# Products of Q's and K's projections accumulated in one PSUM bank, with ScalarE reading the bank between them

## The chip, the cores and the metric

The kernel runs on one core of one Trainium2 chip, all in float32. The metric is the device time of one execution in microseconds. The time before is a median of three runs: 1310.24 us, with 1309.48 and 1314.11 us as the lowest and the highest.

An engine's instructions run in the order of its queue. TensorE (PE in the profile) multiplies into PSUM, which has 8 banks here, each holding one 128x512 float32 tile. VectorE (DVE) and ScalarE (ACT) read PSUM; GpSimd (POOL) works on tiles in SBUF only. The loads and stores that matter here are issued by SyncE (SP).

## The reference, cut to what matters

The reference is a transformer block on two sequences of 512 tokens with 512 features: attention with 32 heads of 128, then a small mixture of experts. What the change touches are the first two of the three projections:

```python
xn = _layernorm(x)                    # (2, 512, 512)
q = rms_norm(xn @ Wq + bq, gq)        # (2, 512, 4096)
k = rms_norm(xn @ Wk + bk, gk)        # (2, 512, 4096)
v = xn @ Wv + bv
```

So for each of Q and K a 512 x 4096 weight meets 1024 tokens, a bias is added for each output column, and the squares of every token's 4096 outputs are summed for the norm.

## The kernel before

**The seven products.** `project` (lines 196 to 305) makes Q, and is called again for K. It works in eight chunks `g` of `GH` = 4 heads (512 output columns). In a chunk the product is a 2 x 2 block product: the weight is cut into `a11`, `a12`, `a21`, `a22` (halves of the input features by halves of the columns), and the tokens of the two sequences (`xTs[0]`, `xTs[1]`) are the other 2 x 2 blocks. Seven block products take the place of eight (Strassen's scheme, in Winograd's form). `weight_sums` (line 185) makes the four sums `s1` to `s4` of weight blocks on POOL, one chunk ahead of use; `token_sums` makes `t1` to `t4` once.

**What a product is.** `product(g, i, a, x, j, tag)` (line 214) takes a PSUM tile from `pt` and issues two matmuls into it (`c` = 0, 1), the first with `start`, for head `j` of the two in a column half. Each float32 matmul is two matmul instructions in the profile, so a chunk is 7 products x 2 heads x 2 x 2 = 56 instructions. `pt` (line 75) takes tiles in turn from two rings, "ps" and "aux", of four banks each.

**How the products become four heads for two sequences.** With the products in the order 1, 2, 6, 7, 4, 5, 3, everything twice, for j = 0 and 1:

- ScalarE copies product 1 with the bias to SBUF: `u1` (line 249, Identity).
- VectorE: product 2 + `u1` is head j of sequence 0 (line 252).
- VectorE: `u2` = product 6 + `u1` (line 280), `u3` = product 7 + `step` + `u2` (line 285; `step` is the difference of the biases of heads j+2 and j).
- VectorE: product 4 + `u3` is head j+2 of sequence 0 (line 290); product 5 + `u3` is head j+2 of sequence 1 (line 296); product 5 + `u2` (line 297); product 3 + that is head j of sequence 1 (line 303).

That is 14 additions on VectorE and 2 copies on ScalarE per chunk, and 14 PSUM tiles, each released when its last reader is done.

**What every finished head causes.** `keep_it` (line 230) squares it on ScalarE (line 237) into a tile of the pool `tmp`, which has four buffers, and POOL adds the square to `accq` or `acck` (line 238). SP stores the head to HBM (line 239; `keptq`, `keptk`). Q's heads lie in a pool of five buffers; K's in two pools of five and seven.

**What else runs in this stretch.** During Q, POOL makes sums of V's weights (`value_sums`, lines 331 to 334), and VectorE makes sums of the output weights (`output_sums`, lines 354 to 357). During K, `between()` runs five times per chunk and makes up to two steps of `scale_some` each time: VectorE scales a stored head of Q (line 382), SP stores it again (`keptqs`, line 383), and after every fourth SP loads four more heads (`four_of`, line 377, 1 MB), which needs the four stores from that buffer to have landed. There are 64 such steps. At the start of chunk `g`, `load_next(g + 1)` loads the next weights (line 91, 1 MB, a pool of two buffers) and POOL makes their sums.

**What sets the order.** PE, VectorE, ScalarE and POOL run in the order of the program text (`IN_ORDER`, line 27). SP isn't in that list: the order of its loads and stores is the framework's planner's, by its own estimates of when each is ready.

**The first two chunks of Q** are opened early by `open_chunk(g, "ps")`, while the second sequence is still being normalized; all others by `open_chunk(g)`, where the tag is `None`.

Of the kernel before, what the change touches and what calls it, by code (L numbers as in the profile page):

```python
# [10 lines left out]
AF = mybir.ActivationFunctionType  # L11
ALU = mybir.AluOpType
AX = mybir.AxisListType

P = 128
# [17 lines left out]
def kernel(ctx: ExitStack, tc: tile.TileContext, x, wq, wk, wv, wo, vecs, rows, wbase, gates, bexp, out):  # L33
# [11 lines left out]
    nc = tc.nc  # L45
# [21 lines left out]
    def tt(name):  # L67
        return tmp.tile([P, 512], F32, tag="tmp", name=name)
# [6 lines left out]
    def pt(name, tag=None):  # L75
        if tag is None:
            tag = ("ps", "aux")[turn_of[0] % 2]
            turn_of[0] += 1
        return psum.tile([P, 512], F32, tag=tag, name=name)
# [8 lines left out]
    def load_w(src, name):  # L88

        w = wpool.tile([P, 4, 512], F32, tag="w", name=name)  # L90
        nc.sync.dma_start(out=w, in_=src.rearrange("(c p) f -> p c f", p=P))
        return w
# [92 lines left out]
    def weight_sums(w, name):  # L185

        a11, a12, a21, a22 = w[:, 0:2, 0:256], w[:, 2:4, 0:256], w[:, 0:2, 256:512], w[:, 2:4, 256:512]
        pairs = [vpool.tile([P, 4, 256], F32, tag="v", name=f"s{i}_{name}") for i in range(2)]
        s1, s2, s3, s4 = out = [t[:, i : i + 2] for t in pairs for i in (0, 2)]
        nc.gpsimd.tensor_tensor(s1, a21, a22, ALU.add)  # L190
        nc.gpsimd.tensor_tensor(s2, s1, a11, ALU.subtract)
        nc.gpsimd.tensor_tensor(s3, a11, a21, ALU.subtract)
        nc.gpsimd.tensor_tensor(s4, a12, s2, ALU.subtract)
        return [a11, a12, a22] + out

    def project(xTs, sums, w_src, bias, step, name, pools, keep, accs, parts, between=lambda: None):

        G = H // GH
        begun = set()
        parts = {0: parts}
        opened = {}
        two = range(2)

        def load_next(g):  # L210
            if g < G:
                parts[g] = weight_sums(load_w(w_src[:, ts(g, GH * P)], f"w_{name}{g}"), f"{name}{g}")

        def product(g, i, a, x, j, tag=None):
            ps = pt(f"p{i}_{name}{g}_{j}", tag)
            for c in range(2):
                nc.tensor.matmul(ps, a[:, c, ts(j, P)], x[c], start=(c == 0), stop=(c == 1))  # L217
            return ps

        def column(v, g, j):  # L220
            return v[:, g * GH + j : g * GH + j + 1]

        def tile_of(what, g, j):
            return opool.tile([P, 512], F32, tag="o", name=f"{what}_{name}{g}_{j}")

        def head(g, b, j):
            pool, tag = pools[j // 2 if len(pools) > 1 else 0]
            return pool.tile([P, 512], F32, tag=tag, name=f"{name}{b}_{g * GH + j}")

        def keep_it(o, g, b, j):  # L230
            h = g * GH + j
            if b not in begun:
                begun.add(b)
                nc.scalar.activation(accs[b], o, AF.Square)
            else:
                sq = tt(f"sq_{name}{b}_{h}")
                nc.scalar.activation(sq, o, AF.Square)  # L237
                nc.gpsimd.tensor_tensor(accs[b], accs[b], sq, ALU.add)  # L238
            nc.sync.dma_start(out=keep[b, h], in_=o)

        def open_chunk(g, tag=None):
            a11, a12 = parts[g][0:2]
            ps1 = [product(g, 1, a11, xTs[0][0:2], j, tag) for j in two]
            ps2 = [product(g, 2, a12, xTs[0][2:4], j, tag) for j in two]
            u1 = opened[g] = [tile_of("u1", g, j) for j in two]

            def leave():
                for j in two:
                    nc.scalar.activation(u1[j], ps1[j], AF.Identity, bias=column(bias, g, j), scale=1.0)
                for j in two:  # L250
                    o = head(g, 0, j)
                    nc.vector.tensor_tensor(o, ps2[j], u1[j], ALU.add)
                    keep_it(o, g, 0, j)

            return leave

        if len(xTs) < B:
            load_next(1)
            leave = open_chunk(0, "ps")
            second = norm_transposed(xs[1], "a1", "aux")  # L260
            leave()
            xTs.append(second())
            leave = open_chunk(1, "ps")
            sums.extend(token_sums(xTs))
            leave()
        t1, t2, t3, t4 = sums
        for g in range(G):
            if g + 1 not in parts:
                load_next(g + 1)
            a11, a12, a22, s1, s2, s3, s4 = parts.pop(g)  # L270
            if g not in opened:
                parts[g] = (a11, a12)
                open_chunk(g)()
                del parts[g]
            u1 = opened.pop(g)
            between()
            u2 = [tile_of("u2", g, j) for j in two]
            for j in two:
                ps = product(g, 6, s2, t2, j)
                nc.vector.tensor_tensor(u2[j], ps, u1[j], ALU.add)  # L280
            between()
            u3 = [tile_of("u3", g, j) for j in two]
            for j in two:
                ps = product(g, 7, s3, t3, j)
                nc.vector.scalar_tensor_tensor(u3[j], ps, column(step, g, j), u2[j], ALU.add, ALU.add)
            between()
            for j in two:
                ps = product(g, 4, a22, t4, j)
                o = head(g, 0, j + 2)
                nc.vector.tensor_tensor(o, ps, u3[j], ALU.add)  # L290
                keep_it(o, g, 0, j + 2)
            between()
            for j in two:
                ps = product(g, 5, s1, t1, j)
                o = head(g, 1, j + 2)
                nc.vector.tensor_tensor(o, ps, u3[j], ALU.add)
                nc.vector.tensor_tensor(u2[j], ps, u2[j], ALU.add)
                keep_it(o, g, 1, j + 2)
            between()
            for j in two:  # L300
                ps = product(g, 3, s4, xTs[1][2:4], j)
                o = head(g, 1, j)
                nc.vector.tensor_tensor(o, ps, u2[j], ALU.add)
                keep_it(o, g, 1, j)
            yield g

# [678 lines left out]
```

## Time and profile before

| What | Value | Where |
|---|---|---|
| Median of the three runs | 1310.24 us (1309.48, 1310.24, 1314.11) | the times |
| Span of the profiled execution | 1306.8 us, mean granted clock 0.996 | the page, first and last instruction; the page gives no other time for this execution |
| PE busy over the span | 1281.5 us (98%) | the page, part 1 |
| DVE, ACT, POOL busy | 982.1, 541.4, 496.8 us (75%, 41%, 38%) | the page, part 1 |
| Q's projection from its third chunk on | 62.2 to 206.6 us | the timeline of PE |
| K's projection | 206.6 to 400.5 us | the timeline of PE |

The span counts from the first to the last instruction of the profiled execution; the median of the runs lies 3.4 us above it. In the timeline a line has the start, the duration, the engine, the line of the kernel, the operation, the output and input tiles and a count; in brackets stands the idle time ahead of it and what ended that. In the table of stretches there are, for each stretch, its length, then the busy time of PE, PEld (weight loads), DVE, ACT and POOL with instruction counts, then the granted clock of PE, the busy share of the DMA engines and their GB/s. In the groups a line has the total busy time, the mean duration of one, and the idle time ahead with what ended it.

A PE that is shown busy is not always a PE at its pace: matmuls overlap, and their durations (592 ns) are longer than their distance (3.43 us for eight, 0.429 us each).

### The profile page before, as it was taken

How to read it: one execution, taken by the hardware profiler on the slowest of the kernel's cores; microseconds unless marked ns; L12 is line 12 of the kernel's file. 1: busy time of each engine (PE TensorE's matmuls, PEld its weight loads, DVE VectorE, ACT ScalarE, POOL GpSimd, SP SyncE). 2: the span in 40 equal slices, each digit the busy share in tenths (PEclk: the TensorE clock that was granted, in tenths of full speed). 3: DMA queues.
4: the chain of work that ended last, by engine and by line, in shares of the span. 5: the costliest groups of instructions: out<-in, count | busy, mean ns of one | idle time of the engine just before them, and what ended most of it. 6: DMA issues, size and time to landing. Idle time of an engine off the chain costs nothing.

```text
span 1306.8 us, 11743 instructions
## 1 busy us (share of the span) xinstructions
PE 1281.5 (98%) x3518; PEld 654.9 (50%) x3518; DVE 982.1 (75%) x1208; ACT 541.4 (41%) x746; POOL 496.8 (38%) x382
## 2 busy tenths in 40 slices
PE   7999999999999999999999999999999999999987
PEld 4444444444444444455555555555555555555453
DVE  7565665888765477888787787878778888888865
ACT  5222222322221144344545445454544556555343
POOL 4789897556763011111122222323223233332102
PEclk9999999999999999999999999999999999999999
DMA  7799979699997765534465566576566565643301
GB/s 291 250 321 311 337 278 312 221 335 330 313 341 266 255 189 183 175 129 129 129 173 174 140 191 165 135 196 170 153 162 184 129 169 129 170 97 81 89 1 64
DMA packets 150335, 257.01 MB, mean 197 GB/s; under 512 B 12160, under 2 KB 41728, under 8 KB 150272
## 3 DMA queue, kind: packets, MB, share of 16 engines
q1 hardware_dynamic: 137312, 232.67, 53.2%
q0 software_dynamic: 12096, 22.03, 10.2%
q10 hardware_dynamic: 864, 1.57, 0.3%
q8 instruction: 28, 0.46, 0.1%
q14 instruction: 35, 0.29, 0.1%
HBM read 149.26 MB, written 84.93 MB: 179 GB/s over the span
## 4 chain that ended last, share of the span: by engine, by line
PE 95%; DVE 2%; DMA 1%; ACT 1%; issue 0%; SPq 0%; ACTq 0%
PE ps L531 17%; PE o L589 17%; PE aux L460 15%; PE p_k L217 15%; PE p_q L217 14%; PE aux L646 12%; PE psy L692 2%; PE f L864 1%; DMA w_q<-in_wq 1%; DMA wo<-in_wo 1%; ACT s L580 1%; PE f L920 1%; PE hg L857 0%; PE aux L563 0%; ACT n_f L157 0%
## 5 line engine op out<-in xcount | busy, mean ns | idle before, releaser
L544 POOL PARTITION_ALL_REDUCE top<-m x64 | 122.2, 1910 | 606.6 <-DVE m L542 606.6
L532 ACT ACTIVATE s<-ps,rk 128x512 f32<-128x512 f32 x256 | 175.8, 687 | 308.5 <-PE ps L531 287.3
L589 PE MATMUL o<-s,v 128*128 128x512 f32 x512 | 230.6, 593 | 3.4 <-ACT s L580 3.4
L531 PE MATMUL ps<-qh,kh 128*128 128x512 f32 x512 | 230.2, 592 | 0.0
L531 PEld LDWEIGHTS ps<-qh,kh 128*128 128x128 f32 x512 | 97.3, 190 | 122.5 <-issue 120.8
L589 PEld LDWEIGHTS o<-s,v 128*128 128x128 f32 x512 | 97.0, 190 | 103.8 <-issue 95.7
L550 DVE TRANSPOSE_TENSOR_REDUCE quarters<-s 128x64 f32<-128x2048 f32 x64 | 147.2, 2300 | 0.0
L577 DVE TENSOR_TENSOR s<-s,top 128x2048 f32<-128x2048 f32 x64 | 146.0, 2282 | 0.0
L541 DVE TENSOR_TENSOR m<-s 128x1024 f32<-128x1024 f32 x64 | 78.0, 1219 | 62.0 <-ACT s L532 62.0
L580 ACT ACTIVATE s<-s 128x2048 f32<-128x2048 f32 x64 | 121.7, 1902 | 5.0 <-DVE s L577 5.0
L460 PE MATMUL aux<-w_v,t 128*128 128x512 f32 x256 | 115.8, 596 | 0.0
L646 PE MATMUL aux<-wr,oh 128*128 128x256 f32 x448 | 103.0, 380 | 0.0
L646 PEld LDWEIGHTS aux<-wr,oh 128*128 128x128 f32 x448 | 84.6, 190 | 23.2 <-issue 12.9
L237 ACT ACTIVATE sq_q<-q 128x512 f32<-128x512 f32 x62 | 38.9, 631 | 135.1 <-DVE q L290 68.1
L238 POOL TENSOR_TENSOR accq<-accq,sq_q 128x512 f32<-128x512 f32 x62 | 81.0, 1308 | 36.1 <-ACT sq_q L237 34.1
L238 POOL TENSOR_TENSOR acck<-acck,sq_k 128x512 f32<-128x512 f32 x62 | 86.2, 1394 | 20.6 <-ACT sq_k L237 17.4
L237 ACT ACTIVATE sq_k<-k 128x512 f32<-128x512 f32 x62 | 38.7, 630 | 132.3 <-DVE k L290 65.4
L460 PE MATMUL aux<-w_v,nT_a 128*128 128x512 f32 x192 | 87.5, 596 | 0.0
L217 PE MATMUL p_k<-t,s_k 128*128 128x512 f32 x192 | 85.0, 592 | 0.0
L217 PE MATMUL p_q<-t,s_q 128*128 128x512 f32 x192 | 85.0, 592 | 0.0
L646 PE MATMUL aux<-wr,s_o 128*128 128x256 f32 x336 | 77.4, 380 | 0.0
L460 PEld LDWEIGHTS aux<-w_v,t 128*128 128x128 f32 x256 | 47.6, 190 | 55.0 <-issue 54.3
(185 smaller groups left out, 1713.0 us busy)
## 6 DMA issues: line engine op xcount, KB each, us to landing
keptq<-q SPq DMA_DIRECT2D x64, 256.0 KB, 6.9
q<-keptq SPq DMA_DIRECT2D x16, 1024.0 KB, 6.4
keptk<-k SPq DMA_DIRECT2D x64, 256.0 KB, 6.5
w_v<-keptw SPq DMA_DIRECT2D x32, 512.0 KB, 3.9
keptqs<-q SPq DMA_DIRECT2D x64, 256.0 KB, 6.6
qh<-keptqs SPq DMA_DIRECT2D x64, 256.0 KB, 3.0
kh<-keptk SPq DMA_DIRECT2D x64, 256.0 KB, 2.7
keptv<-o_v SPq DMA_DIRECT2D x64, 256.0 KB, 3.1
```

The costliest lines, as they stand in the source:

```text
L217: nc.tensor.matmul(ps, a[:, c, ts(j, P)], x[c], start=(c == 0), stop=(c == 1))
L238: nc.gpsimd.tensor_tensor(accs[b], accs[b], sq, ALU.add)
L460: nc.tensor.matmul(ps, x[c][:, ts(t, P)], w[:, c, :], start=(c == 0), stop=(c == 1))
L531: nc.tensor.matmul(ps, kk[i][:, ts(k, P)], qs[i], start=True, stop=True)
L532: nc.scalar.activation(s[:, k, :], ps, AF.Copy, scale=rks[b][:, k : k + 1])
L541: nc.vector.tensor_tensor(m, s[:, 0:2, :], s[:, 2:4, :], ALU.max)
L544: nc.gpsimd.partition_all_reduce(ms[i], m[:, 0, :], P, ReduceOp.max)
L550: nc.vector.tensor_reduce(quarters.rearrange("p k j -> p (k j)"), ss[i].rearrange("p k (j r) -> p (k j) r", r=32), AX.X, ALU.add, apply_tr ...
L577: nc.vector.tensor_tensor(s, s, top.unsqueeze(1).to_broadcast([P, NT, 512]), ALU.subtract)
L580: nc.scalar.activation(ss[i], ss[i], AF.Exp)
L589: nc.tensor.matmul(po, vs[b, c][:, k, ts(j, P)], ss[i][:, k, :], start=(k == 0), stop=(k == NT - 1))
L646: nc.tensor.matmul(ps[:, t, :], a, right_of[i, g][:, j, :], start=(j == 0), stop=(j == 1))
```

## The change

`product` may be given a tile to accumulate onto (`onto`): then its first matmul carries no `start`. In the chunks that are opened without a tag, products 1, 6, 7 and 4 accumulate in the bank of product 1, and ScalarE reads the bank after each of them with the right bias: `u1`, `u2`, `u3` and head j+2 of sequence 0. Product 3 accumulates onto product 5's bank. VectorE keeps three additions per head pair: product 2 + `u1`, product 5 + `u3`, and (5 + 3) + `u2`. The order of the products becomes 1, 2, 6, 5, 7, 4, 3. A chunk takes 6 PSUM tiles, 6 additions on VectorE and 8 copies on ScalarE; squares, stores and matmuls are as many as before. In the first two chunks of Q, `chain` is `None`: there products 6, 7 and 4 share a bank, and VectorE reads it.

```diff
-        def product(g, i, a, x, j, tag=None):
-            ps = pt(f"p{i}_{name}{g}_{j}", tag)
+        def product(g, i, a, x, j, tag=None, onto=None):
+            ps = pt(f"p{i}_{name}{g}_{j}", tag) if onto is None else onto
             for c in range(2):
-                nc.tensor.matmul(ps, a[:, c, ts(j, P)], x[c], start=(c == 0), stop=(c == 1))
+                first = c == 0 and onto is None
+                nc.tensor.matmul(ps, a[:, c, ts(j, P)], x[c], start=first, stop=(c == 1), skip_group_check=True)
             return ps
...
-            u1 = opened[g] = [tile_of("u1", g, j) for j in two]
+            u1 = [tile_of("u1", g, j) for j in two]
+            opened[g] = u1, ps1 if tag is None else None
...
-            u1 = opened.pop(g)
+            u1, chain = opened.pop(g)
+
+            def copied(what, ps, j, shift):
+                u = tile_of(what, g, j)
+                if chain is not None:
+                    nc.scalar.activation(u, ps, AF.Identity, bias=column(bias, g, j + shift), scale=1.0)
+                elif shift:
+                    nc.vector.scalar_tensor_tensor(u, ps, column(step, g, j), u1[j], ALU.add, ALU.add)
+                else:
+                    nc.vector.tensor_tensor(u, ps, u1[j], ALU.add)
+                return u
+
             between()
-            u2 = [tile_of("u2", g, j) for j in two]
+            sum6 = [product(g, 6, s2, t2, j, onto=chain and chain[j]) for j in two]
+            u2 = [copied("u2", sum6[j], j, 0) for j in two]
+            between()
+            ps5 = [product(g, 5, s1, t1, j) for j in two]
+            between()
+            sum7 = [product(g, 7, s3, t3, j, onto=sum6[j]) for j in two]
+            u3 = [copied("u3", sum7[j], j, 2) for j in two]
             for j in two:
-                ps = product(g, 6, s2, t2, j)
-                nc.vector.tensor_tensor(u2[j], ps, u1[j], ALU.add)
-            between()
-            u3 = [tile_of("u3", g, j) for j in two]
-            for j in two:
-                ps = product(g, 7, s3, t3, j)
-                nc.vector.scalar_tensor_tensor(u3[j], ps, column(step, g, j), u2[j], ALU.add, ALU.add)
+                o = head(g, 1, j + 2)
+                nc.vector.tensor_tensor(o, ps5[j], u3[j], ALU.add)
+                keep_it(o, g, 1, j + 2)
             between()
             for j in two:
-                ps = product(g, 4, a22, t4, j)
+                product(g, 4, a22, t4, j, onto=sum7[j])
                 o = head(g, 0, j + 2)
-                nc.vector.tensor_tensor(o, ps, u3[j], ALU.add)
+                if chain is not None:
+                    nc.scalar.activation(o, sum7[j], AF.Identity, bias=column(bias, g, j + 2), scale=1.0)
+                else:
+                    nc.vector.scalar_tensor_tensor(o, sum7[j], column(step, g, j), u1[j], ALU.add, ALU.add)
                 keep_it(o, g, 0, j + 2)
             between()
             for j in two:
-                ps = product(g, 5, s1, t1, j)
-                o = head(g, 1, j + 2)
-                nc.vector.tensor_tensor(o, ps, u3[j], ALU.add)
-                nc.vector.tensor_tensor(u2[j], ps, u2[j], ALU.add)
-                keep_it(o, g, 1, j + 2)
-            between()
-            for j in two:
-                ps = product(g, 3, s4, xTs[1][2:4], j)
+                product(g, 3, s4, xTs[1][2:4], j, onto=ps5[j])
                 o = head(g, 1, j)
-                nc.vector.tensor_tensor(o, ps, u2[j], ALU.add)
+                nc.vector.tensor_tensor(o, ps5[j], u2[j], ALU.add)
                 keep_it(o, g, 1, j)
```

## The prediction, made before the changed kernel was run

> **What bounds the kernel now.** I read first the chain of waits from the start to the end of K's projection (start, duration, engine, tile, line, count), since it shows whether the stretch that is changed waits for anything.
>
> ```profile
> 20.98 185.58 PE p_q L217 x432
> 206.56 24.03 PE p_k L217 x56
> 230.59 1.72 PE ssq L412 x4
> 232.31 168.23 PE p_k L217 x392
> 400.54 5.15 PE aux L460 x12
> ```
>
> From 20.98 to 400.54 us the chain is PE alone. 56 instructions take 24.03 us, 0.429 each, and 392 take 168.23, again 0.429: every chunk runs at one pace, K's as Q's, though VectorE's load differs. The table of stretches says the same:
>
> ```profile
> 170.00:180.00 10.00, 10.00 (x25) 4.48 (x24) 4.98 (x8) 1.92 (x4) 9.74 (x8) 1.00 0.97 280
> 270.00:280.00 10.00, 10.00 (x25) 4.48 (x24) 9.88 (x10) 1.86 (x3) 9.31 (x7) 1.00 1.01 326
> ```
>
> PE is busy throughout; VectorE is half idle in Q and full in K (9.88 of 10 us), and PE doesn't mind. The DMA engines are full too (0.97 and 1.01). So VectorE's 75% of the span is not the limit here, and taking work from it can't shorten a chunk. The question is only whether the change makes PE wait.
>
> **What is removed and added.** The groups of Q's stretch have the prices (total, then mean ns):
>
> ```profile
> L280 DVE TENSOR_TENSOR u_q<-p_q,u_q 128x512 f32<-128x512 f32 x12 | 8.3, 690 | 9.5 <-PE p_q L217 9.5
> L285 DVE SCALAR_TENSOR_TENSOR u_q<-p_q,steps,u_q 128x512 f32<-128x512 f32 x12 | 9.0, 751 | 12.0 <-PE p_q L217 12.0
> L249 ACT ACTIVATE u_q<-p_q,vec 128x512 f32<-128x512 f32 x12 | 8.0, 680 | 3.1 <-PE p_q L217 3.1
> ```
>
> In 14 of 16 chunks VectorE loses 8 additions (lines 280, 285, 290, 297: 2 x (0.69 + 0.75 + 0.69 + 0.68) = 5.6 us per chunk, 79 us in all) and ScalarE gains 6 copies (6 x 0.68 = 4.1 us, 57 us). ScalarE then has 8 x 0.68 + 8 squares x 0.63 = 10.5 us of a chunk's 24.03: room enough. In Q's first two chunks VectorE goes from 14 to 12 additions. Matmuls are as many. Direct gain on the path: 0. The chain excludes more: nothing but PE is on it.
>
> **The new waits on PE.** Products 6, 7 and 4 now wait until ScalarE has read the bank, 3 until VectorE has. Behind such a wait stands all of PE's queue. A product pair takes 8 instructions, 3.43 us, so by the time from a chunk's start (0): 1 from 0, 2 from 3.43, 6 from 6.87, 5 from 10.30, 7 from 13.73, 4 from 17.17, 3 from 20.60. The handoffs come from the timeline:
>
> ```profile
> 19.45 0.81 ACT L157 ACTIVATE n_a<-x,shift_a,rs_a 128x512 f32<-128x512 f32 x1 [0.42 <-DMA wo<-in_wo]
> 20.32 0.42 PEld L159 LDWEIGHTS nt_a<-ident,n_a 128*128 128x128 f32 x4 [0.31 <-ACT n_a L157]
> 113.90 0.69 ACT L249 ACTIVATE u_q<-p_q,vec 128x512 f32<-128x512 f32 x1 [0.37 <-PE p_q L217]
> ```
>
> ScalarE to PE: 20.26 to 20.32, 0.06 us. PE to ScalarE: product 1 of the chunk that starts at 110.27 ends at 113.70, the copy starts at 113.90, 0.20 us. The tightest round trip is 7, `u3`, 4: 7 for the first head ends at 15.45, `u3` runs from 15.65 to 16.34, PE may go at 16.40 and wants to at 17.17, or at 16.74 if its weight load (0.43 us ahead in the timeline) has to wait as well. Spare: 0.3 to 0.8 us, so 0; if the trip were 0.5 us longer than these rows, up to 0.2 us per chunk, 3 us in 14 chunks. `u2` has 2.6 us to spare, product 3 more than 3 us. Banks: 6 tiles per chunk in rings of 8, each ring coming round after a chunk and a third; 0. The first two chunks, with VectorE in the loop: `u2` is done near 32.2 us and 7 starts at 34.73; 0.
>
> A rule against this change is in the Trainium skill, ScalarE: Activation LUTs, "Rules for kernel authors": additions belong on VectorE, which is up to about 3x faster in bf16. The rows here are float32 and say 0.68 us against 0.69. An estimate by the rule's factor, 3 x 0.69 = 2.07 us for `u3`, would overrun the spare time by about 1 us per chunk, 14 us in all; by the rows it is 0.
>
> **Where ScalarE is late.** ScalarE is in order, so `u1` stands behind the squares of the chunk before. A square needs a buffer of `tmp` (four), which POOL frees; POOL, in order too, stands before `weight_sums`, which wait for 1 MB of weights. In K's last chunks this already happens:
>
> ```profile
> 365.50 0.67 SPq L91 DMA_DIRECT2D w_k<-in_wk  x1
> ...
> 375.72 1.76 POOL L190 TENSOR_TENSOR s_k<-w_k 128x512 f32<-128x512 f32 x1 [11.38 <-DMA w_k<-in_wk]
> ...
> 381.23 14.22 POOL L238 TENSOR_TENSOR acck<-acck,sq_k 128x512 f32<-128x512 f32 x10
> ...
> 382.52 0.63 ACT L237 ACTIVATE sq_k<-k 128x512 f32<-128x512 f32 x1 [11.42 <-POOL acck L238]
> ```
>
> POOL waits 11.38 us for the weights, ScalarE 11.42 us for POOL. `u1` of the last chunk (line 249) follows at 387.09, 10.6 us after the chunk's start (376.50). Before, only VectorE waited for it; now product 6, due at 383.37, does. The four squares left over need four additions of POOL: 381.23 + 4 x 1.42 + 0.1 + 0.63 = 387.6, `u1` until 388.3, so product 6 would start 5.0 us late. The same sum for the two chunks before: sums done at 328.97 and 352.22, product 6 possible 7.2 us later, at 336.2 and 359.4; due at 335.3 and 359.3: 0.9 and 0.1 us. These don't add up: time that PE lost earlier comes off what it loses later. So 5.0 us with all other times unchanged.
>
> Two things take from it. VectorE no longer blocks POOL so much (POOL's addition is 1.27 us where it is alone, 1.42 here: 4 x 0.15, and some 0.5 over the four sums, 1 us together). And the traffic of K, which fills the DMA engines from about 255 us, can begin earlier: VectorE's first scalings no longer stand among additions (0 to 3 us). One thing adds: SP's order is the planner's, and product 4, which frees the weights' buffer, is now sixth and not fifth (3.43 us later). If the planner puts the load one pair of stores later, past a load that waits for landings (3.5 to 4.5 us in SP's timeline), the sums come 2 to 6 us later. Bounds: 5.0 - 4 = 1, or 0 if a wait further up is lifted, to 5.0 + 6 = 11. I take 3, nearer to the unchanged row less its reliefs.
>
> At the joint of Q and K, VectorE's first head of K waits until 217.43 for POOL's sums of V's weights. Its squares on ScalarE (to 219.4) now stand ahead of `u2`, done at 220.1, and 7 is due at 220.3. Q's last store chain may be 0.9 us later, as head j+2 of sequence 1 is now third in its five buffers: 0 to 0.9 us, and it comes off the 3 later.
>
> **Sum.** 1306.8 (span) + 0 (additions) + 0 (round trips) + 3 (K's `u1`) = about 1310 us of span; the runs' median lies 3.4 above the span, so 1313 us. What is behind K, the values and attention, isn't changed.
>
> **Rivals.**
> (a) *K paced by SP and DMA: slower.* The weight loads of K's chunks 3 to 7 start at 261.83, 287.96, 314.12, 339.07 and 365.50: one per 25.9 us, against 24.03 of PE. Now PE hangs on that pace through `u1`. Place: product 6 in the last three chunks; price: the full bound of 11 us, 1321; it decides once the last sums are done later than about 383 us. For: DMA shares near 1. Against: the reliefs, and that the lag is bounded by what K's stores and loads need anyway.
> (b) *The round trips are longer than the rows: slower.* One overrun per chunk, 14 times; 0.5 us of it makes 7 us, 1317. Against: 0.3 to 0.8 us spare.
> (c) *Nothing waits: unchanged, 1310.* For: squares wait less as POOL speeds up.
> (d) *The relief of VectorE shortens K: faster.* At most what PE idles before 400 us after its start, which the chain has as 0, so only a shift of loads elsewhere could give it; 1303 would take 7 us from the start or the tail, which don't change.
>
> The Trainium skill, TensorE: Matmul & The Clock Gate, "A second HAM failure mode: psum-queue depth-cycling", says that short PE idles between groups that cycle through banks can throttle the clock again. The granted clock here is 1.00 in every stretch before 1256 us, so no run here shows it; an estimate by that page, with each throttled stretch half its time lost, would put several us on top of (a) or (b).
>
> **How the numbers follow.** A measurement of this kernel tells about 0.5% (6.5 us) from no change. Unchanged within that, 0.61: my forecast (0.41, 0.5 to 6.5 us lost) with (c) (0.20). Slower, 0.34: (a) 0.23, (b) 0.11. Faster (d), 0.05. The time is the forecast's, 1313. The range takes the lower end from (c), less 2 us of the runs' own scatter, 1308, and the upper from (a), 1321.
>
> **What would show it.** After: additions on VectorE 6 per chunk, VectorE's busy time down by about 80 us, ScalarE's up by 57. The chain through Q still PE alone, 24.03 us per chunk (the round trips). In K a PE or weight load waiting for ScalarE at line 249 or the read of `u1`, in the last two or three chunks, behind POOL and `w_k`; K's end at 401 to 407 us and the rest of the span shifted by as much. Wrong would be: gaps ahead of product 4 in each chunk (b); K's end past 408 (a); a K that ends before 400 (d).

## The result, and the profile after

| | before | after |
|---|---|---|
| Median of the runs | 1309.86 us (1307.83 to 1314.11, 4 runs) | 1320.87 us (1318.36 to 1323.11, 4 runs) |
| Span of the profiled execution | 1306.8 us | 1321.3 us |
| K's projection ends | 400.5 us | 415.8 us |

The ratio is 1.0075, with a 95% interval from 1.0052 to 1.0097: the change costs 0.5 to 1%, some 11 us. The profiled execution of after took 1323.11 us, the longest of the four, and its span grew by 14.5 us; the medians differ by 11.0. So the sums below, which are made against the profiled execution, explain 3.5 us more than the medians show. The kernel before scatters as well: beside the experiments it ran 23 or 24 times each, with medians from 1310.92 to 1312.58 us, and against these the changed kernel loses 8 to 10 us.

The first part of the changed kernel's page (busy time, share of the span, instructions):

```profile
PE 1286.6 (97%) x3518; PEld 655.5 (50%) x3518; DVE 905.1 (69%) x1092; ACT 593.3 (45%) x830; POOL 493.0 (37%) x382
```

VectorE lost 77 us of work (from 982.1) and ScalarE gained 52 (from 541.4), as the change says. The time went the other way. The chain of waits of the changed kernel, in K's second half (start, duration, what, line, count), cut to its main pieces, where the kernel before had one piece of PE alone from 232.31 to 400.54:

```profile
321.40 9.34 DMA w_k<-in_wk
330.88 1.28 POOL s_k L190
...
342.47 10.53 PE p_k L218 x20
354.57 8.37 DMA keptqs<-q
...
375.58 9.44 DMA w_k<-in_wk
...
394.07 1.27 POOL acck L239
396.72 19.10 PE p_k L218 x40
415.82 5.15 PE aux L471 x12
```

Read its second part downwards: a store lands (354.57), SP gets on and loads weights, POOL makes their sums and adds squares, and only then PE goes on. Twice PE hangs on the end of that chain, at 342.47 and at 396.72. The timeline of PE in the changed kernel (start, duration, engine, line, operation, tiles, count, idle time ahead) has these two and a third:

```profile
216.19 12.23 PE L218 MATMUL p_k<-t,s_k 128*128 128x512 f32 x24 [2.21 <-ACT u_k L251]
243.71 10.46 PE L218 MATMUL p_k<-t,s_k 128*128 128x512 f32 x24
342.47 12.23 PE L218 MATMUL p_k<-t,s_k 128*128 128x512 f32 x24 [2.46 <-ACT u_k L251]
396.72 12.23 PE L218 MATMUL p_k<-t,s_k 128*128 128x512 f32 x24 [4.25 <-ACT u_k L251]
```

Each is product 6 waiting for ScalarE's `u1` (line 251 now): in K's first chunk, at the joint with Q, and in K's sixth and last. Together they are 8.9 us. But the 24 instructions behind such a wait take 12.23 us, where those of an undisturbed chunk (243.71) take 10.46: 1.77 us more, three times, 5.3 us. The table of stretches says why (length, busy times, then the granted clock of PE, the share of the DMA engines and GB/s):

```profile
216.00:220.00 4.00, 3.81 (x6) 1.66 (x7) 3.35 (x3) 0.62 (x2) 3.92 (x3) 0.62 0.90 353
222.00:338.00 116.00, 116.00 (x271) 51.31 (x271) 66.75 (x72) 47.73 (x77) 70.45 (x53) 1.00 0.83 286
396.00:400.00 4.00, 3.28 (x5) 1.35 (x6) 3.39 (x4) 2.99 (x5) 3.84 (x4) 0.73 1.05 406
```

Right behind each wait the granted clock is down; between them it is 1.00. The records of the clock show half speed for 3.41 us after each of the three. So 8.9 us of waits and 5.3 us of half clock make 14.2 us. Matmuls overlap (592 ns long, 429 apart), so PE still counts as busy for the first 0.16 us of each wait: 0.5 us more. K's projection is 14.7 us longer, 208.7 against 194.0. It also begins 0.55 us later (207.11 against 206.56): Q's six chunks took 0.8 us more (145.03 against 144.20), from a start 0.3 us earlier. So K ends 15.3 us later, and the span grew by only 14.5, since what follows K took 0.8 us less.

Why `u1` is late in the last chunk, in the timelines of POOL and ScalarE of the changed kernel:

```profile
385.15 1.27 POOL L190 TENSOR_TENSOR s_k<-w_k 128x512 f32<-128x512 f32 x1 [13.06 <-DMA w_k<-in_wk]
390.16 14.53 POOL L239 TENSOR_TENSOR acck<-acck,sq_k 128x512 f32<-128x512 f32 x10
391.45 0.63 ACT L238 ACTIVATE sq_k<-k 128x512 f32<-128x512 f32 x1 [9.97 <-POOL acck L239]
395.90 1.25 ACT L251 ACTIVATE u_k<-p_k,vec 128x512 f32<-128x512 f32 x2
```

This is the chain that the prediction drew: POOL waits 13.06 us for weights, ScalarE's square 9.97 us for a buffer that POOL has to free, and `u1` stands behind the squares. At the joint it is another one, in the timelines of VectorE and ScalarE of the changed kernel:

```profile
214.05 0.69 DVE L314 TENSOR_TENSOR q<-p_q,u_q 128x512 f32<-128x512 f32 x1 [7.92 <-PE p_k L218]
214.84 0.63 ACT L238 ACTIVATE sq_q<-q 128x512 f32<-128x512 f32 x1 [7.99 <-DVE q L314]
215.38 1.25 ACT L251 ACTIVATE u_k<-p_k,vec 128x512 f32<-128x512 f32 x2
```

Q's last head is added up at 214.05 and not at 209.68 as before; its square and with it `u1` are 4.4 us later. The wait is put down to PE, which had long been done with that product. In the timeline of before the same addition waits for the store of an older head (`keptq`) to land and free one of the five buffers:

```profile
209.68 0.69 DVE L303 TENSOR_TENSOR q<-p_q,u_q 128x512 f32<-128x512 f32 x1 [4.05 <-DMA keptq<-q]
```

So it does in the first experiment below, at 214.37 after 8.27 us. ScalarE stands still for 7.99 us with K's first copy queued behind the square. Where the 4.4 us come from stands in SP's queue, of before first, then of the changed kernel:

```profile
193.05 0.32 SPq L336 DMA_DIRECT2D keptw<-a_v  x1
...
202.75 0.77 SPq L239 DMA_DIRECT2D keptq<-q  x1
```

```profile
197.25 0.32 SPq L347 DMA_DIRECT2D keptw<-a_v  x1
...
207.41 1.60 SPq L240 DMA_DIRECT2D keptq<-q  x3
```

The store that frees the buffer is issued at 207.41 and not at 202.75 (it lands at 213.93, before at 209.56). It stands in SP's queue behind the stores of the sums of V's weights (`keptw`), which come 4.2 us later, since POOL makes these sums 4.2 us later (at 195.96 and not at 191.76). POOL in turn had just waited for the square of the last head of the chunk before (2.15 us) and for K's weights (0.75 us). So a late last head makes the next chunk's last head late, by way of its square, POOL and SP.

### The profile page after: what moved, and what is told of

Same layout as the page of the kernel before. It is cut to its first block, busy times and chain, and to the rows that moved or that the text cites. A ratio compares the mean times of both kernels' runs of the same rounds, so it can differ in the third digit from the quotient of the medians.

```text
span 1321.3 us, 11607 instructions
## 1 busy us (share of the span) xinstructions
PE 1286.6 (97%) x3518; PEld 655.5 (50%) x3518; DVE 905.1 (69%) x1092; ACT 593.3 (45%) x830; POOL 493.0 (37%) x382
## 3 DMA queue, kind: packets, MB, share of 16 engines
q0 software_dynamic: 12096, 22.03, 10.2%
## 4 chain that ended last, share of the span: by engine, by line
PE 88%; DMA 4%; DVE 3%; ACT 2%; POOL 1%; issue 1%; SPq 0%; ACTq 0%; POOLq 0%; DVEq 0%
PE ps L542 17%; PE o L600 16%; PE aux L471 15%; PE p_q L218 13%; PE aux L657 12%; PE p_k L218 9%; PE psy L703 2%; DMA w_k<-in_wk 1%; PE f L875 1%; DVE q L393 1%; POOL acck L239 1%; DMA keptk<-k 1%; DMA keptqs<-q 1%; DMA keptq<-q 1%; ACT s L591 1%
## 5 line engine op out<-in xcount | busy, mean ns | idle before, releaser
L218 PE MATMUL p_k<-t,s_k 128*128 128x512 f32 x192 | 89.0, 622 | 8.9 <-ACT u_k L251 8.9
L663 ACT COPY w<-aux 128x512 f32<-128x512 f32 x84 | 47.8, 581 | 59.3 <-PE aux L657 47.6
```

What stands on the lines that cost most here:

```text
L218: nc.tensor.matmul(ps, a[:, c, ts(j, P)], x[c], start=first, stop=(c == 1), skip_group_check=True)
```

## The experiments

The theory (A): nothing is wrong with reading the bank between products; PE now waits for ScalarE's queue, in which `u1` stands behind squares, and these hang on POOL, late weights and, at the joint, on a late store. Rivals: the stream of weights itself is the limit, by SP and the DMA engines, whatever ScalarE does (B); the round trips between PE and ScalarE in each chunk cost time (C).

**Product 5 ahead of 6**, which gives `u1` 3.43 us more and `u2` as much less.

```diff
             between()
+            ps5 = [product(g, 5, s1, t1, j) for j in two]
+            between()
             sum6 = [product(g, 6, s2, t2, j, onto=chain and chain[j]) for j in two]
             u2 = [copied("u2", sum6[j], j, 0) for j in two]
             between()
-            ps5 = [product(g, 5, s1, t1, j) for j in two]
-            between()
             sum7 = [product(g, 7, s3, t3, j, onto=sum6[j]) for j in two]
```

> Product 5, which waits for nothing, is put ahead of product 6, so that ScalarE's copy u1 is due 3.43 us later in each chunk. Theory A (PE waits at product 6 for u1, which stands behind squares on ScalarE, and each wait of over 2 us is followed by 3.41 us at half clock): the waits of 2.4, 2.6 and 4.4 us become 0, 0 and about 1 us, no half clock in Q and K, K ends near 402 us; 1310 to 1312 us. Rival B (K is paced by SP and the DMA engines, whatever PE waits for): the waits move to another product, K ends near 415 us, 1318 to 1322 us. Rival C (the round trips PE, ScalarE, PE cost in each chunk): one more tight trip (6, u2, 7) in each chunk, not faster than 1321 us.

Measured: 1316.7 us (1314.38 to 1321.09), ratio 1.0044 (1.0026 to 1.0061). PE's timeline of this kernel:

```profile
224.85 5.29 PE L218 MATMUL p_k<-t,s_k 128*128 128x512 f32 x8 [4.42 <-ACT u_k L282]
395.43 7.11 PE L218 MATMUL p_k<-t,s_k 128*128 128x512 f32 x16 [1.10 <-ACT u_k L251]
```

In the last chunk 1.10 us is left of 4.25, as expected, and the wait in the sixth chunk is gone; 0.84 us at product 1 of the last chunk, for its weights, is new. At the joint the wait is lifted at product 6 and comes back larger at product 7, which stands behind `u2` (line 282): the slack was only moved. Half a miss: the time lies between the ranges of A and B.

**Sixteen buffers for the squares** in place of four:

```diff
-                sq = tt(f"sq_{name}{b}_{h}")
+                sq = opool.tile([P, 512], F32, tag="o", name=f"sq_{name}{b}_{h}")
```

> The squares go into the pool of 16 buffers that the copies use and no longer into tmp's 4, so ScalarE doesn't wait for POOL. Theory A: the waits of K's last chunks (2.6 + 4.4 us) and the half clock after them (2 x 1.7 us) go, the one at the joint of Q and K (2.4 + 1.7 us, due to a store of Q that has not landed) stays: 1311 to 1314 us. Rival B: unchanged, 1318 to 1322 us. Rival C: unchanged as well.

Measured: 1312.52 us (1311.73 to 1314.32), ratio 1.0002 (0.9985 to 1.0018): the loss is gone. PE's timeline of this kernel has waits over 0.5 us at the joint alone, this one at product 6 and 1.08 us at product 7, neither with half clock behind it:

```profile
216.76 7.11 PE L218 MATMUL p_k<-t,s_k 128*128 128x512 f32 x16 [2.01 <-ACT u_k L251]
```

POOL still waits for the last weights (10.14 us, 13.06 in the changed kernel), and PE isn't hurt. For A, against B and C.

**K's weights loaded through ScalarE's queue**, issued behind product 4 of the chunk that lets go of their buffer:

```diff
+            if name == "k" and g + 2 < G:
+                early[g + 2] = load_w(w_src[:, ts(g + 2, GH * P)], f"w_{name}{g + 2}", nc.scalar)
```

> K's weights are loaded through ScalarE's queue, right after product 4 has read the buffer, and not at the place that the planner gives them on SP. Theory A with the late weights as its root: POOL no longer waits up to 13 us for them, its additions come on time, the waits of K's last chunks go and the joint's stays: 1311 to 1315 us. If tmp's four buffers are too few even with weights on time, or if K is paced by the DMA engines (rival B): K's waits stay, 1318 to 1322 us.

Measured: 1319.28 us (1314.36 to 1322.43), ratio 1.0057 (1.0035 to 1.0079). A miss, with a new wait. The waits of ScalarE in this kernel's second half of K (what waited, for what, in total, times, longest), and PE's timeline:

```profile
ACT sq_k L242 <- DMA keptqs<-q: 8.2, 1, 8.2
```

```profile
368.93 12.23 PE L222 MATMUL p_k<-t,s_k 128*128 128x512 f32 x24 [3.30 <-ACT u_k L255]
```

The square at 367.06 stood right behind the load issued at 366.59 and started 8.2 us late; the profile names stores of the DMA queues as what ended it. ScalarE paid for the load's issue, and PE for ScalarE. PE also waits 1.84 and 1.23 us at the joint and 1.30 us at product 3 of the chunk before this wait, and POOL still up to 8.7 us for weights. The run tells that ScalarE's queue is the sore place, not whether the weights' lateness alone is.

**The squares of products 4 and 3 behind the next chunk's `u1`** on ScalarE (four buffers, as in the changed kernel; in the program a head's store now stands ahead of its square):

```diff
+            if later:
+                late.append(lambda: square(o, b, h))
+            else:
+                square(o, b, h)
...
                     nc.scalar.activation(u1[j], ps1[j], AF.Identity, bias=column(bias, g, j), scale=1.0)
+                while late:
+                    late.pop(0)()
```

> The squares of products 4 and 3 are put behind the next chunk's u1 on ScalarE (also from Q into K); tmp keeps four buffers, weights and product order stay. Theory A: u1 waits for nothing but product 1 and one copy; all three waits at product 6 go, the joint's too, and at most u2 in the last chunk is late: 1310 to 1313 us. Rivals B and C: 1318 to 1322 us.

Measured: 1421.46 us (1419.25 to 1423.29), ratio 1.0833 (1.0798 to 1.0868). A large miss. PE's waits in this kernel, from 20 to 430 us:

```profile
PE p_q L220 <- ACT u_q L293: 37.1, 6, 9.5
PE p_k L220 <- ACT u_k L293: 26.0, 3, 11.0
```

The additions of the late squares came to stand behind `weight_sums` in POOL's queue, which here waits up to 18.3 us for weights; the squares hold the four buffers as long, and now `u2` stands behind them in chunk after chunk. Whether a reader's queue is short matters less than what it hangs on.

**The change in Q alone** and **in K alone**; the other projection is the code of before:

```diff
+            if name == "q":
                 sum6 = [product(g, 6, s2, t2, j, onto=chain and chain[j]) for j in two]
...
+            else:
+                u2 = [tile_of("u2", g, j) for j in two]
```

> The change in Q's projection alone; K's chunks run as before. Theory A (product 6 waits for u1 behind squares that POOL holds up in K, and at the joint): Q has the round trips but none of the waits, so unchanged, 1309 to 1313 us, no PE wait over 0.5 us before 400 us. Rival C (the round trips themselves cost): 6 of 14 chunks, so some 4 to 5 of the 11 us, 1314 to 1316 us.

> The change in K's projection alone; Q's chunks run as before, with head j+2 of sequence 1 fifth and not third to be stored. Theory A: the joint's wait is short (u1 of K's first chunk at 211 us as before, u2 less than 1 us late), the two waits of K's last chunks and the half clock after them stay: 1316 to 1320 us. If the joint's wait is K's alone and not due to Q's order of stores: the full loss, 1319 to 1323 us. Rival C: 8 of 14 chunks, some 6 us, 1316 us, with gaps in every chunk of K.

Measured: Q alone 1312.81 us (1308.14 to 1316.56), ratio 0.9999 (0.9981 to 1.0017); K alone 1313.86 us (1311.08 to 1315.15), ratio 1.0011 (0.9998 to 1.0024). C falls with Q: six chunks of round trips cost nothing. K alone costs about 1 us, which can't be told from nothing, where I had expected most of the loss; the parts don't add up to 11. PE's timeline, of K alone first, then of Q alone:

```profile
386.95 12.23 PE L218 MATMUL p_k<-t,s_k 128*128 128x512 f32 x24 [3.23 <-ACT u_k L251]
```

```profile
381.86 9.32 PE L218 MATMUL p_k<-nT_a,w_k 128*128 128x512 f32 x16 [4.95 <-DVE q L424]
```

K alone has no wait at the joint and one wait less later on; the one it has, 3.23 us, is near the 3 us of the prediction's sum, and half clock follows it. Its loads of weights are issued where those of before are (the last at 365.93 us, before at 365.50, in the changed kernel at 375.58). The joint's wait needs both: the changed Q, whose last head is late (213.51 with Q alone, 209.86 with K alone), and K's new dependence on ScalarE. And the profile of Q alone shows something about K as it was: unchanged, it can lose 4.95 us at product 1 of the last chunk, with half clock behind it. The profile names VectorE, but the load of the weights lands at 381.73, and POOL, which starts on them at the same 381.86, names this load. This execution (1315.5 us) is one of the longer of the ten. K as it was is itself on the edge of its weights.

**Matmuls that nobody reads ahead of product 6** in K's first, sixth and last chunk (2, 2 and 4 of them, 1.7, 1.7 and 3.4 us), so that PE does not idle while it waits:

```diff
+            fill = {0: 2, 5: 2, 7: 4}.get(g, 0) if name == "k" else 0
+            for _ in range(fill):
+                nc.tensor.matmul(spare, a12[:, 0, ts(0, P)], xTs[0][2], start=True, stop=True)
```

> Matmuls that nobody reads are put ahead of product 6 in K's chunks 0, 5 and 7: 2, 2 and 4 of 0.86 us each, so 1.7, 1.7 and 3.4 us, in the place where PE waits for u1 (2.4, 2.6 and 4.4 us). The result is the same. If the half clock after the waits is caused by PE's idling and costs 1.7 us each: idle shrinks below 1 us, no half clock in Q and K, 1314 to 1317 us, 4 to 5 us below the change. If the slow rows after the waits have another cause (late operands, the bank): unchanged, 1319 to 1322 us.

Measured: 1319.96 us (1318.46 to 1321.85), ratio 1.0055 (1.0036 to 1.0074). The stretches of this kernel that hold the first and the last of the three waits:

```profile
210.00:230.00 20.00, 18.51 (x43) 7.82 (x42) 7.87 (x9) 6.09 (x10) 14.11 (x11) 1.00 0.91 333
392.00:404.00 12.00, 10.90 (x26) 4.61 (x25) 6.98 (x6) 5.80 (x10) 11.69 (x9) 1.00 1.05 401
```

The clock stays at 1.00 all through Q and K: the idle time had lowered it. The time, though, is a miss, and lies where the other cause was expected: K ends at 413.62 us against 415.82, so 2.2 us were won and not 5.3, and the medians differ by 0.9 us. PE waits elsewhere instead: 1.24 us at product 7 of K's first chunk (for `u2`), 0.97 us at product 1 of the last chunk, whose weights were not there, and still 1.10 us behind its four filling matmuls.

**The kernel before, with one wait of PE put in** before product 7's turn in 14 chunks, of lengths from 1 to 3.5 us (copies on ScalarE, and a small matmul that reads the last):

> The kernel before, with one PE wait in each of 14 chunks, ahead of product 7, made by 1 to 3 copies on ScalarE of different width that a one-column matmul needs: planned idle of about 1.3 (twice), 1.5 (twice), 1.6, 1.7 (twice), 2.0 (twice), 2.1, 2.2, 2.3, 2.5 and 2.9 us. It measures the disputed cost by itself. If the clock falls by the share of idle time in a window of 3.41 us: gaps of 2.2 us and more within one window are followed by 3.41 us at half clock, those below about 2.0 us are not; each half-clock window costs 1.7 us on top of its gap, so the span grows by the sum of the gaps (about 27 us) plus 1.7 us for each. If idling does not cause it, the span grows by the gaps alone and the clock stays at 1.00.

Measured: one execution of 1350.54 us, span 1348.7. PE's timeline of this kernel at two of the waits:

```profile
179.83 0.48 PE L290 MATMUL idle_q<-idle_q,ident 128*128 128x1 f32 x2 [1.87 <-ACT idle_q L287]
180.18 5.28 PE L219 MATMUL p_q<-t,s_q 128*128 128x512 f32 x8
...
263.30 0.38 PE L290 MATMUL idle_k<-idle_k,ident 128*128 128x1 f32 x2 [3.07 <-ACT idle_k L287]
263.54 3.68 PE L219 MATMUL p_k<-t,s_k 128*128 128x512 f32 x8
```

Eight instructions take 5.28 us behind a wait of 1.87 us, and 3.68 us behind one of 3.07. Six of the 14 waits (1.76, 1.76, 1.87, 1.98, 2.16 and 3.46 us) are followed by half clock; 2.08 and 3.07 are not, nor the six of 1.06 to 1.44. So it is not the length alone, and the lower limit of about 2.0 us that I had expected doesn't hold. The span grew by 41.9 us: the waits are 25.5 of it and the half clock 10.2; the rest, 6 us, is not taken apart. More of this at the end.

**All squares behind `u1` and `u2`, with sixteen buffers:** no copy that product 6 or 7 waits for stands behind a square; `u3`, for product 4, still does. A head's store stands ahead of its square here too.

```diff
+            late.append(lambda: square(o, b, h))
...
             u2 = [copied("u2", sum6[j], j, 0) for j in two]
+            squares()
```

> The changed kernel with two edits: the squares get opool's sixteen buffers, and on ScalarE every square is queued behind u1 and u2 of the chunk that follows (and behind u3), so that no copy that PE waits for stands behind a square. If ScalarE's queue (copies behind squares) is the whole cause of the 10 us: the wait at u1 at the joint of Q and K (2.4 us in the changed kernel, 2.0 with more buffers alone) goes too, no wait of PE over 0.3 us at u1 or u2 is left in Q and K, no spell at half clock there; time 1308 to 1312, as the kernel before. It isn't faster than before by more than 2 us, since PE's 24.03 us per chunk is the bound of Q and K in both and VectorE's relief is worth nothing. If VectorE's relief is worth something once the waits are gone: under 1305. If something other than the squares in ScalarE's queue holds u1 back (the landing of weights, POOL): waits of 2 to 4 us stay at product 6 or move to product 1, 1314 to 1320.

Measured: 1316.1 us (1310.17 to 1320.88), ratio 1.0028 (1.001 to 1.0045). A miss against the forecast of 1308 to 1312. No wait for `u1` or `u2` is left in K (in Q, 1.83 us for `u3` at product 4 of the seventh chunk); but see PE's and POOL's timeline of this kernel:

```profile
383.46 9.94 PE L220 MATMUL p_k<-nT_a,w_k 128*128 128x512 f32 x16 [4.38 <-DMA w_k<-in_wk]
```

```profile
383.55 1.26 POOL L190 TENSOR_TENSOR s_k<-w_k 128x512 f32<-128x512 f32 x1 [14.56 <-DMA w_k<-in_wk]
```

PE itself waits for the last weights now, at product 1, as in the run with Q alone changed, whose K is that of before; here as there a spell of 6.83 us at half clock goes with it. So B is half right: behind ScalarE's queue stands the weights' lateness, and A alone doesn't account for all.

**Product 5 first and sixteen buffers together:**

> The changed kernel with product 5 ahead of 6 (3.43 us more for u1, 3.43 less for u2) and the squares in opool's sixteen buffers, their place in ScalarE's queue unchanged. If the waits at u1 come from the squares' buffers and the waits at u2 from squares of K's first head that stand ahead of u2: the last chunk's wait (1.1 us with product 5 first alone) goes, the wait at the joint stays at product 7 (4.4 us with product 5 first alone, of which VectorE's wait for POOL's sums of V's weights makes most), with one spell at half clock (1.7 us) at most; time 1313 to 1316. If more buffers clear the joint too: 1308 to 1312.

Measured: 1314.65 us (1313.28 to 1317.03), ratio 1.0025 (1.0012 to 1.0037), as A has it. One wait is left, 3.73 us at product 7 of K's first chunk (for `u2`), with half clock behind it.

**Three buffers for weights** (and 12 for `opool`, to make room): a load no longer waits for product 4 of the chunk before.

```diff
-    opool = ctx.enter_context(tc.tile_pool(name="opool", bufs=16))
+    opool = ctx.enter_context(tc.tile_pool(name="opool", bufs=12))
-    wpool = ctx.enter_context(tc.tile_pool(name="wpool", bufs=2))
+    wpool = ctx.enter_context(tc.tile_pool(name="wpool", bufs=3))
```

> The changed kernel with three buffers for weights in place of two (opool gets 12 tiles in place of 16 to make room), so that a load of K's weights no longer waits until product 4 of the chunk before has let go of the buffer and can stand earlier in SP's queue. If K's waits come from the late weights (they hold POOL, POOL holds the squares, the squares hold u1): POOL's waits for weights in K, 10 to 13 us in the changed kernel, shrink to under 5 us; the waits at product 6 of K's sixth and last chunk go; the wait at the joint, 2 to 2.4 us, stays with its one spell at half clock at most; time 1311 to 1314. If the lag of the weights is a matter of DMA bandwidth (shares near 1) and not of SP's order and the two buffers: the extra megabyte in flight delays the stores, the waits stay or move, 1317 to 1321.

Measured: 1312.43 us (1309.9 to 1314.11), ratio 0.9996 (0.9983 to 1.0008). POOL's waits ahead of the sums of weights from 200 to 420 us in the changed kernel (the second line names PE, though the later of its two ends with the landing of a load, issued at 347.32 and down at 354.59), then all of POOL's waits with three buffers:

```profile
POOL s_k L190 <- DMA w_k<-in_wk: 35.2, 3, 13.1
POOL s_k L190 <- PE p_k L218: 16.1, 2, 8.4
```

```profile
POOL acck L239 <- ACT sq_k L238: 53.6, 21, 8.1
POOL accq L239 <- ACT sq_q L238: 5.4, 1, 5.4
```

POOL no longer waits for weights at all, and PE's waits in the sixth and last chunk are gone; the joint keeps 0.54 and 1.24 us, without half clock. The same megabytes cross the same DMA engines: the lateness was SP's order and two buffers, not the bandwidth. With the run of sixteen buffers, that settles A against B: ScalarE's queue is where PE is hurt, and in K's later chunks the late weights are what fills it.

**The same, with the squares of product 3 behind the next chunk's `u1`:**

```diff
-                keep_it(o, g, 1, j)
+                keep_it(o, g, 1, j, g + 1 not in opened and (name == "q" or g + 1 < G))
```

> As the kernel with three buffers for weights, and the squares of the heads of product 3, which come last in a chunk, are queued on ScalarE behind the next chunk's u1. If the wait at the joint comes from these squares (a head of Q that waits for a store's landing holds its square, and the square holds u1): it goes, and no wait of PE over 0.5 us is left in Q and K; 1308 to 1311, as before the change. It is not under 1305 if PE's own 24.03 us per chunk is the bound. If POOL's sums of weights, which now stand ahead of these squares' additions, hold the four buffers as they did where the late squares were tried with two buffers for weights: waits at u2, over 1316.

Measured: 1308.35 us (1307.12 to 1308.99, 12 runs), against 1312.51 us (1308.8 to 1316.42, 23 runs) of the kernel before beside it: ratio 0.9969 (0.9957 to 0.998). Its chain of waits:

```profile
20.67 185.53 PE p_q L220 x432
206.20 24.03 PE p_k L220 x56
230.24 1.72 PE ssq L433 x4
231.95 168.23 PE p_k L220 x392
400.19 5.15 PE aux L481 x12
```

This is the chain of before, piece by piece: PE alone, 0.429 us per instruction, K's end at 400.19 against 400.54. All of the loss is gone. The joint's loop is cut as well: V's sums no longer stand behind the square of the last head, they are stored from 189.77 us on (196.09 with three buffers alone), and Q's last head is added up at 209.00 (212.60). It is 0.3% faster than before, and its 12 runs lie within 1.9 us, the 23 of before within 7.6. A likely reason is that the old K now and then runs out of weights, as the profile of Q alone shows, and that half clock follows: of the 93 executions of the kernel before beside the experiments, the 16 with a mean granted clock of 0.994 took 1314.76 us or more and the 46 with 0.996 or 0.997 at most 1311.91, while this kernel's 12 all have 0.996 or 0.997. It was not tried by itself. The kernel before with three buffers was not run, so how much of the 0.3% belongs to the buffers, and whether the change itself has any part in it, stays open; VectorE's relief does not show, since the chunks are as long.

## Why the prediction was right, and where it was wrong

The time landed within 0.2 us of the upper end of the range, at the price of rival (a), and not at the forecast of 1313; two of the four runs lie above the range. By the prediction's own bound of 6.5 us it is slower, to which it gave 0.34. That the range held is in part luck: its end was the bound for one late `u1` behind late weights, and what filled it were three shorter waits, one of them with another cause, and a clock that the sum left out. The step from span to time, 3.4 us, mixed two executions: in the runs that list both, the time is 1.8 to 2.2 us above the span.

- **VectorE's relief is worth 0.** Right: the chunks that wait for nothing take 24.03 us in both kernels, and the chain of the last experiment is that of before.
- **The round trips are worth 0; rival (b).** Right: Q, where there are six chunks of them, took 0.8 us longer, the one wait listed (0.26 us) is for `u1` and not for a round trip, and the change in Q alone measured 0.9999. The warning of the Trainium skill, ScalarE: Activation LUTs, "Rules for kernel authors", did not bite in float32: `u3` took 0.69 us and kept within its spare time.
- **`u1` in K's last chunks.** The mechanism and place were right, weights to POOL to squares to `u1`. With unchanged times I had 5.0 us for the last chunk and 0.9 for the sixth; waits of 4.25 and 2.46 were measured, and 3.23 in the last chunk alone where the joint's wait was missing (K alone).
- **"These don't add up: time that PE lost earlier comes off what it loses later."** This is the step that failed. It would hold if the late load stood still while PE slipped towards it. It doesn't: a load needs the buffer that PE frees with product 4, and SP's queue needs heads that PE makes. K's loads were issued 8.1, 3.9, 5.5, 7.3, 8.3 and 10.1 us later than before, while PE was 4.7 us behind after the joint and fell back by 4.4 more in the sixth chunk. So the three waits add up to 8.9 us, where the sum had 3. The change in K alone shows the other side: without the joint's wait the last load keeps its time and one wait of 3.23 us is all that is left.
- **The joint, "0 to 0.9 us, and it comes off the 3 later".** I looked at `u2`, behind squares of K's first head. That wait exists (4.42 us with product 5 first), but it was hidden here, since product 6 waited first: `u1` itself stands behind the square of Q's last head, which comes 4.4 us later, not 0.9. In the timeline of before that square runs at 210.47 and `u1` until 212.25, 1.2 us ahead of product 6, so 0.9 us would have been free and 4.4 us are not. I counted the head's own place in the five buffers; what I left out is that its store stands in SP's queue behind V's sums, and these in POOL's behind the squares of the chunk before. Neither part alone makes this wait; I costed Q's stores and K's copies one by one.
- **The reliefs, 1 to 4 us.** In the changed kernel they did not come. POOL's additions behind the weights take 1.45 us each (14.53 for ten) against 1.42, and the loads of weights come later.
- **The clock.** The sum had no term for it; the prediction had it outside the sum, as an estimate of "several us on top", for want of a row. It is 5.3 us of the 14.5, the largest missing term. Reading the bank between products did not lower the clock by itself: in Q it stayed at 1.00. The Trainium skill, TensorE: Matmul & The Clock Gate, Part 1: The HAM clock gate (the "warmup" mystery), names an idle window of about 3.4 us as what lowers the clock; here idle times of 2.21 and 2.46 us were enough.
- **Rival (a), K paced by SP and DMA.** Its sign came: the sums were done at 390.2 us, past the 383 from which I had it decide, and K ended past 408. Its price, 11 us of late sums at product 6 of the last three chunks, is the loss of the medians by coincidence: the waits there are 6.7 us, the rest is the joint and the clock. Of its cause the first half holds, SP's order with two buffers; the DMA engines' bandwidth does not, as three buffers showed.

## What to carry to other kernels

Moving work off an engine that isn't the bound gained nothing here, but a new reader between two matmuls of a bank ties PE to everything that stands ahead of that reader in its engine's queue, so follow that queue back (squares, their buffers, POOL, weights, stores) before counting durations. Waits of an engine that also drives the loads it waits for do add up, and here an idle time of about 2 us on PE could cost 1.7 us more by the clock. When parts measured alone come to nothing and together to 11 us, look at the place where the one's late output meets the other's new dependence.

## What the runs showed of the hardware

The granted clock of PE falls to half after quite short idle times, for a fixed time: every spell at half clock in Q and K in these runs lasted 3.41 us or twice or three times that (three times in the kernel of 1421 us), and each 3.41 us cost about 1.7 us (1.77 behind the waits of the changed kernel, 1.68 behind the wait of 1.87 us above). In the kernel with 14 waits, idle times of 1.76 us could lower it while one of 3.07 us did not.

The spells start on a fixed grid. In the changed kernel they begin at 216.95, 343.24 and 397.85 us, 37 and 16 times 3.413 us apart; in the kernel with 14 waits at 152.68, 179.99, 292.63, 319.94, 374.55 and 401.86, which are 8, 33, 8, 16 and 8 times 3.413 us apart. On the grid of that kernel the wait of 3.07 us falls into two windows:

```profile
258.49:261.90 3.41, 1.74 (x5) 0.43 (x3) 3.41 (x5) 0.57 (x2) 2.86 (x2) 1.00 0.76 282
261.90:265.31 3.41, 2.01 (x6) 1.09 (x7) 0.93 (x2) 1.28 (x3) 0.00 (x0) 1.00 0.68 229
265.31:268.72 3.41, 3.41 (x9) 1.52 (x8) 2.21 (x4) 0.00 (x0) 0.00 (x0) 1.00 0.63 197
```

PE is idle for 1.7 us of the first and 1.4 us of the second, and the clock stays at 1.00. Likewise the last wait of the changed kernel, 4.25 us, has 1.97 us in one window, with the next still at 1.00, and 2.28 us in that next one, behind which the clock is at half. So what counts is the idle time within one window, and an idle time split over two can go free. In Q and K of all these runs, no window at full clock with up to 1.70 us of idle time was followed by half clock, and each with 2.06 us or more was. In between both happen: four windows with 1.76 to 1.98 us (in the kernel with 14 waits) were followed by it, and one with 1.97 (the changed kernel) and one with 2.00 (sixteen buffers) were not. So some 2 us is a fit to these runs, not a measured threshold. The Trainium skill, TensorE: Matmul & The Clock Gate, Part 1: The HAM clock gate (the "warmup" mystery), calls the window free-running and 3413 ns long, which agrees.
